# Bidirectional minGRU stack, fusion and ternary FFN on one Trainium2 core: first pair reordered, VectorE's order in the fusion slots turned round, the last projections done tile by tile

## The chip, the cores and the metric

The kernel runs on one core of a Trainium2 chip, in one launch. The metric is the device time in microseconds; below its value in repeated runs is given as a median. A separate profiled execution gave the span, the rows and the waits that are quoted. TensorE is called PE, VectorE DVE, ScalarE ACT, GpSimd POOL and SyncE SP.

## What is computed

The input x is 8 batches of 512 tokens by 512 features, float32. Each batch goes through two stacks of four minGRU layers, one reading the tokens forward and one backward. A layer computes a gate and a candidate by matrix products, and a linear scan over the tokens; from the second layer on the input is added, and each layer ends in a LayerNorm over the features:

```python
def _mingru(x, Wz, bz, Wh, bh):
    z = jax.nn.sigmoid(jnp.einsum('bsi,hi->bsh', x, Wz) + bz)
    h_tilde = jnp.tanh(jnp.einsum('bsi,hi->bsh', x, Wh) + bh)
    a = jnp.clip(1.0 - z, CLAMP_LO, CLAMP_HI)
    return _linear_scan(a, z * h_tilde)          # h[s] = a[s] * h[s-1] + z[s] * h_tilde[s]
```

The two results are put side by side, multiplied by a fusion matrix (512 by 1024), a bias is added, and the batch's own x is added to it. The input of the stacks is the LayerNorm of x over the features. The FFN behind it is

```python
    h = jnp.einsum('btd,hd->bth', layernorm_no_affine(x), absmean(W_fc))     # ternary weights
    h = layernorm(jax.nn.gelu(h, approximate=False), ln_w, ln_b)
    return x + jnp.einsum('bth,dh->btd', h, absmean(W_proj))
```

(shortened here), where `absmean` divides a matrix by its mean absolute value and rounds to -1, 0 or 1. It has 2048 hidden features, and the output is 8 by 512 by 512.

The call of the stacks passes the same matrix and bias for gate and candidate and for both directions, so a layer of a stream needs one product per 128 features.

## The kernel before, in words

**First part, the recurrence (lines 200 to 720).** The batches are worked off in four pairs (b, b+1); a pair has four streams s = (batch, direction), and each of the layers 1 to 3 is done for the four streams in turn. Features lie on the partitions, in four chunks `o` of 128. For one chunk, PE makes `u` (line 416, four float32 matmuls of 128x512, in one of four `ps_u` buffers), ACT makes a, t and z (`factors`, lines 433 to 435), DVE clamps a (439), multiplies z and t (440), scans (444) and adds the input (496). Layer 0 (`first_layer`, lines 449 to 479) is shared by the two directions: its `u` is scaled by a row of token scales (466), and DVE runs both the forward scan zf and the backward scan z.

A LayerNorm (`norm`) needs token statistics, so PE transposes a stream to tokens by features (`pt`, line 293, one of two `ps_t` buffers), DVE takes bn_stats (149) and two or three small operations (151, 155, 160), POOL takes a power (156), ACT makes `nmr` (166) and the normalised `tok` (167), which frees the `ps_t` buffer; PE then transposes back (`pf`, line 302, one of two `ps_f` buffers), and ACT applies gamma and beta (308). After layer 3 only the scale is needed, and the chain ends with the statistics (`norm_last`). `norm_x` takes the statistics of x itself.

**Who goes when.** The order of every engine is written by a small planner. `slot(work, cap)` is one time step: the PE work given to it; due "factors"; then `shares(cap)`, which takes pieces from the queue `turns` (transpose and statistics) and from the queue `backs` (transpose back), up to two of each, the second only where `cap` is 2 or it is late; then the statistics of x (`x_shares`); due "scans"; the work's own end; due "resid"; and the functions that the shares left for the end (ACT's `tok` and affine). `now` counts slots. Each engine runs what it is given in order.

**The first pair** starts with `norm_x`, the products that center the first weights (`pm`), eight slots of `first_layer` for batches 0 and 1, and two slots with `fold_sums` (`pfold`, line 611). After layer 1 of the batch 1 streams come slots of their own for `fold` (`pm`, line 627, and four DVE multiplies of the fusion weights, line 632) and `fold_bias` (`pb`, line 638).

**A fusion stage** ends each pair (`fusion`, lines 514 to 545). For each of four token tiles DVE adds the bias row to x (525), PE makes `pu` of both directions (530, eight matmuls), and DVE adds both to it, scaled by the tokens' rs (538); SP stores the row. Between the tiles stand the first layers of the next pair. A list `extra` holds pieces of the weights' quantisation, two DVE operations each (171 and 172); in the fusion stages `pieces(1 + t % 2)` works one or two off after each tile's slot. `combined` (line 597) splits the two FFN LayerNorm rows in four DVE operations, when the last pair starts.

**Second part, the FFN (from line 742).** For each batch and each of 16 hidden chunks k, `fc` makes eight matmuls (781), ACT the GELU (785), a square (787) and a scaled copy (789), and DVE two sums (796) and the rest `glo` (798); `proj` follows two chunks behind (808, eight matmuls into four `po` tiles). After the last chunk `token_stats` (819 to 831) reduces the sums to a token scale; for the last batch four `center` operations (841) and four final ones (854) on DVE end the work, and SP stores each tile.

Of the kernel before, what the change touches and what calls it, by code (L numbers as in the profile page):

```python
# [24 lines left out]
def kernel(  # L25
# [90 lines left out]
    nc.vector.memset(warm, 0.0)  # L116

# [7 lines left out]
    load_xT(1)  # L125
    for t in range(NT):
        load_x("n", 1, t)
    nc.sync.dma_start(out=gam, in_=gamma)
# [78 lines left out]
    with rec:  # L207
# [28 lines left out]
        def shares(cap):  # L236
# [3 lines left out]
            for q in (turns, backs):  # L240
                some = []
                for i in range(2):
                    if not q or not ready(q[0][0]):
                        break
                    at, piece = q[0][:2]
                    late = (at.at if isinstance(at, Tokens) else at) + piece < now[0]
                    if i >= cap and not late:
                        break
                    some.append(take(q))
                last = some + last  # L250
# [36 lines left out]
        def turned(zs, t, name, frees=0):  # L287
            def source():
                if t == NT - 1:
                    zlive[0] -= frees  # L290
                pt = ps_t.tile([P, H], F32, tag="pt", name=f"pt_{name}")
# [25 lines left out]
        def norm(s, zs, tag, pause):  # L317
# [8 lines left out]
            for t in range(NT):  # L326
                queue(turns, s, at, t, tokens(turned(zs, t, f"{tag}_{t}", NC_), toks, None, f"{tag}_{t}"))
            for c in range(NC_):
                queue(backs, s, toks, c, back(toks, dst, c, True, f"{tag}_{c}"))
# [69 lines left out]
        def slot(work=None, cap=1):  # L399
            end = work() if work is not None else None  # L400
            due("factors")
            last = shares(cap) + x_shares()
# [43 lines left out]
        def first_layer(b, lag=0):  # L446
# [4 lines left out]
            def chunk(o):  # L451
                def work():
# [11 lines left out]
                    def scaled():  # L464
# [4 lines left out]
                        def scans():  # L469
# [3 lines left out]
                            scan(z, a, z, True)  # L473
                            zf.append(f)
                            zb.append(z)
                            if o == NC_ - 1:
                                state[b, 0] = xT.pop(b)
                                norm((b, 0), zf, f"{b}0_0", 1)
                                norm((b, 1), zb, f"{b}1_0", 1)
# [5 lines left out]
        def layer(s, l):  # L485
# [5 lines left out]
            for o in range(NC_):  # L491
# [14 lines left out]
                if s[0] < 2 and (l == L - 1 or o % 2) and len(extra) > 2 * NW:  # L506
# [8 lines left out]
        def fusion(b):  # L515
            hs, rs = [], []

            def tile_of(t):
                def work():
# [5 lines left out]
                    nc.vector.tensor_tensor(row, row, fb, ALU.add)  # L525
                    pus = []
# [69 lines left out]
        def combined():  # L596
# [3 lines left out]
            for i, v in enumerate((lnw, lnb)):  # L600
                hi, lo = rows["comb"][:, :, 2 * i, :], rows["comb"][:, :, 2 * i + 1, :]
                v = v.unsqueeze(2).broadcast_to([P, NF, 32])
                nc.vector.tensor_copy(hi, v)
                nc.vector.tensor_tensor(lo, v, hi.bitcast(F32), ALU.subtract)


        def fold_sums(d):
# [7 lines left out]

            def end():
                folded[d] = tokp.tile([P, H], F32, tag="tok", name=f"fold_{d}")
                held[0] += 1
                nc.scalar.copy(folded[d], ps)
            return end  # L620

        folded = {}

        def fold(d):
# [3 lines left out]

            def end():
                for c in range(NC_):  # L630
                    w = fw[:, d * NC_ + c, :]
                    nc.vector.scalar_tensor_tensor(w, w, gam[:, c : c + 1], pm, ALU.mult, ALU.subtract)
            return end

        def fold_bias():
# [3 lines left out]

            def end():  # L640
                nc.vector.tensor_tensor(fb, pb, fb, ALU.add)
                held[0] -= 2
            return end
# [7 lines left out]
        for b in range(2):  # L651
            norm_x(b, 0)
# [10 lines left out]
        both = const.tile([P, NC_, 2, 64], F32, name="both")  # L663
        picks = []
        for i in range(2):
            s = const.tile([P, P], F32, name=f"fpick{i}")
            nc.vector.memset(s, 0.0)
            nc.vector.memset(s[64 * i : 64 * i + 1, :], 1.0 / H if i else 1.0)
            picks.append(s)
        f0, f1 = first_layer(0), first_layer(1, 2)  # L670
        for work in f0:
            slot(work, 2)
        for i, v in enumerate((bet, gam)):
            nc.vector.tensor_copy(both[:, :, i, :], v.unsqueeze(2).broadcast_to([P, NC_, 64]))
        for work in f1:
            slot(work, 2)
        for d in range(2):
            slot(lambda d=d: fold_sums(d), 2)
        for b in range(0, B, 2):
# [11 lines left out]
            for l in range(1, L):  # L691
# [5 lines left out]
                for s in ((b, 0), (b, 1), (b + 1, 0), (b + 1, 1)):  # L697
# [12 lines left out]
                    if s[0] == 1 and l == 1:  # L710
                        slot(lambda d=s[1]: fold(d))
                        if s[1] == 1:
                            slot(fold_bias)
# [5 lines left out]
            for i in range(2):  # L719
                for t, tile_ in enumerate(fusion(b + i)):  # L720
                    slot(tile_, 2)
                    pieces(1 + t % 2)
# [14 lines left out]

    gpool = ctx.enter_context(tc.tile_pool(name="g", bufs=3, reuse_waits="tile"))
    partp = ctx.enter_context(tc.tile_pool(name="parts", bufs=4, reuse_waits="tile"))
# [63 lines left out]
    def proj(b, k, *parts):  # L803
        if k == 0:
            po[b] = [ps_o.tile([P, H], F32, tag=f"po{t}", name=f"po_{b}_{t}") for t in range(NT)]
        for t in range(NT):
# [41 lines left out]
    def finish(b):  # L848

        for t in range(NT):  # L850
            rs = stat[b][0][:, t : t + 1]
            if b == B - 1:
                row = xs["y", b, t]
                nc.vector.scalar_tensor_tensor(row, po[b][t], rs, row, ALU.mult, ALU.add)
                store(b, t)
            else:
                scaled = tokp.tile([P, H], F32, tag="tok", name=f"scaled_{b}_{t}")
                nc.scalar.activation(scaled, po[b][t], AF.Copy, scale=rs)

                def rest(t=t, scaled=scaled):  # L860
                    center(b, t, scaled)
                    store(b, t)
                rests.append(rest)
# [15 lines left out]
    for j in range(B * NF + LAG):  # L879
        b, k = divmod(j, NF)  # L880
        late = []
        if b < B:
            waiting.append((b, k, *fc(b, k)))
# [16 lines left out]
        if b < B:  # L900
            at = 12 if b == 0 else 8
            if at <= k < at + NT:
                xt = xs["y", b, k - at]
                nc.vector.tensor_tensor(xt, xt, rows[1], ALU.add)
            if b + 1 < B:
                if k == 2:
                    load_y(b + 1)
                if k in (6, 7):
                    y_stats(b + 1, (2 * k - 12, 2 * k - 11))
                if k in (8, 9):  # L910
# [44 lines left out]
```

## Time and profile before

| what | value |
|---|---|
| time, median of 3 runs | 1756.46 us (1756.12 to 1757.0) |
| the profiled execution: its time | 1756.91 us |
| its span in the profile | 1754.9 us |
| PE busy | 1713.5 us (98%) |
| DVE busy | 1456.2 us (83%) |
| ACT busy | 1068.7 us (61%) |
| POOL busy | 214.7 us (12%) |
| PE waits for ACT's `tok` before `pt` | 14.4 us in 14 waits |
| PE waits for ACT's `tok` before `pf` | 4.5 us in 3 waits |

A row of the timeline gives the start, the length in us, the engine, the line, the operation, what it writes and reads, the number of records that it holds, and in brackets the engine's idle time before it with the instruction that ended it. A line of the waits gives the engine, the line that waited, what it waited for, the time in all, how often, and the longest. A busy engine is not an engine at its peak: matmuls overlap, and their pace is read from their starts.

### The profile page before, as it was taken

The page shows a single profiled execution, that of the slowest core. Times are in us where ns is not written, and L with a number is a line of the kernel's source. Part 1 is how long each engine was busy: PE and PEld are TensorE (multiplying, and loading weights), DVE is VectorE, ACT ScalarE, POOL GpSimd, SP SyncE. Part 2 cuts the span into 40 slices and gives each one's busy share as a digit, 9 for nine tenths or more (in the row PEclk, how much of TensorE's full clock was granted, in tenths as well). Part 3 has the DMA queues.
Part 4 walks back from the last instruction along what each step waited for, and adds up shares of the span by engine and source line. Part 5 has one row for each costly group of instructions (what it writes and reads, how often), then busy time and mean ns, then how long its engine had stood idle before and what let it go on. Part 6 is the DMA issues. An engine that isn't in the chain of part 4 may idle for free.

```text
span 1754.9 us, 19733 instructions
## 1 busy us (share of the span) xinstructions
PE 1713.5 (98%) x6424; PEld 1043.4 (59%) x6424; DVE 1456.2 (83%) x2865; ACT 1068.7 (61%) x1836; POOL 214.7 (12%) x334
## 2 busy tenths in 40 slices
PE   7989999999999999999999999999999999999998
PEld 3544554455555445555544455554588888888886
DVE  6988989789998988999898899997468778778876
ACT  3887884248887335888623588871256566566653
POOL 1111112111111111111111111111000000000000
PEclk9999999999999999999999999999999999999999
DMA  7002321132000024100002301101301101101100
GB/s 264 13 25 72 102 73 43 54 110 107 1 1 24 19 78 155 61 1 5 20 31 84 114 1 48 73 1 50 119 0 49 42 7 48 49 13 36 49 24 24
DMA packets 46454, 91.73 MB, mean 52 GB/s; under 512 B 5264, under 2 KB 5264, under 8 KB 45328
## 3 DMA queue, kind: packets, MB, share of 16 engines
q1 hardware_dynamic: 45488, 88.91, 15.0%
q10 hardware_dynamic: 864, 1.57, 0.3%
q8 instruction: 50, 0.82, 0.2%
q14 instruction: 52, 0.43, 0.1%
HBM read 65.30 MB, written 25.17 MB: 52 GB/s over the span
## 4 chain that ended last, share of the span: by engine, by line
PE 82%; DVE 10%; issue 4%; ACT 2%; POOL 1%; DMA 0%; DVEq 0%; POOLq 0%
PE u L416 33%; PE ph L781 12%; PE po L808 11%; PE pu L530 11%; PE pt L293 5%; PE u L459 4%; PE pf L302 4%; DVE st L149 2%; DVE z L444 2%; DVE z L440 1%; PE py L192 1%; DVE zf L444 1%; DVE mv L151 1%; ACT tok L167 1%; DVE z L496 1%
## 5 line engine op out<-in xcount | busy, mean ns | idle before, releaser
L416 PE MATMUL u<-xT,gw 128*128 128x512 f32 x768 | 348.8, 597 | 0.0
L416 PE MATMUL u<-h,gw 128*128 128x512 f32 x768 | 346.5, 594 | 0.0
L444 DVE TENSOR_TENSOR_SCAN z<-a,z 128x512 f32<-128x512 f32 x224 | 274.3, 1224 | 7.8
L785 ACT ACTIVATE g<-ph 128x512 f32<-128x512 f32 x128 | 76.4, 597 | 245.6 <-PE ph L781 245.6
L433 ACT ACTIVATE a<-u,ngb 128x512 f32<-128x512 f32 x192 | 131.7, 686 | 153.7 <-PE u L416 152.6
L149 DVE BATCH_NORM_STATS2 st<-pt 128x6 f32<-128x512 f32 x256 | 177.7, 694 | 56.1 <-PE pt L293 55.4
L416 PEld LDWEIGHTS u<-xT,gw 128*128 128x128 f32 x768 | 139.8, 192 | 139.8 <-issue 139.8
L416 PEld LDWEIGHTS u<-h,gw 128*128 128x128 f32 x768 | 139.0, 191 | 138.3 <-issue 138.3
L156 POOL TENSOR_TENSOR rs<-ve,mhalf 128x1 f32<-128x1 f32 x192 | 122.9, 640 | 724.5 <-DVE nmu L160 671.6
L808 PE MATMUL po<-pwq,ghi 128*128 128x512 f32 x512 | 203.5, 397 | 0.0
L781 PE MATMUL ph<-yhi,fcq 128*128 128x512 f32 x512 | 199.7, 390 | 0.0
L808 PE MATMUL po<-pwq,glo 128*128 128x512 f32 x512 | 199.6, 390 | 0.0
L781 PE MATMUL ph<-ylo,fcq 128*128 128x512 f32 x512 | 199.4, 389 | 0.0
L440 DVE TENSOR_TENSOR z<-z,t 128x512 f32<-128x512 f32 x224 | 153.8, 687 | 16.0 <-ACT z L435 15.7
L167 ACT ACTIVATE tok<-pt,nmr,rs 128x512 f32<-128x512 f32 x192 | 149.2, 777 | 6.4
L796 DVE TENSOR_TENSOR acc<-acc,g 128x512 f32<-128x512 f32 x112 | 77.3, 691 | 91.0 <-ACT g L785 90.1
L293 PEld LDWEIGHTS pt<-ident,z 128*128 128x128 f32 x640 | 78.2, 141 | 92.6 <-issue 43.8
L435 ACT ACTIVATE z<-u,gb 128x512 f32<-128x512 f32 x192 | 132.1, 688 | 0.0
L434 ACT ACTIVATE t<-u,gb 128x512 f32<-128x512 f32 x192 | 130.6, 680 | 0.0
L433 ACT ACTIVATE a<-z,ngb 128x512 f32<-128x512 f32 x32 | 23.1, 721 | 166.8 <-DVE z L466 166.6
L302 PE MATMUL pf<-ident,tok 128*128 128x128 f32 x768 | 115.0, 274 | 6.5 <-ACT tok L167 4.5
L459 PE MATMUL u<-xT,gw 128*128 128x512 f32 x256 | 117.3, 605 | 2.2 <-DVE xf L538 1.8
(138 smaller groups left out, 2650.0 us busy)
## 6 DMA issues: line engine op xcount, KB each, us to landing
xn<-in_x_dram SPq DMA_DIRECT2D x32, 256.0 KB, 5.5
xf<-in_x_dram SPq DMA_DIRECT2D x32, 256.0 KB, 5.8
x<-xf SPq DMA_DIRECT2D x32, 256.0 KB, 2.0
xy<-x SPq DMA_DIRECT2D x32, 256.0 KB, 3.7
out_dram<-xy SPq DMA_DIRECT2D x32, 256.0 KB, 2.0
xT<-in_xt_dram SPq DMA_DIRECT2D x7, 1024.0 KB, 7.7
fca<-in_fc_wT_dram SPq DMA_DIRECT2D x16, 256.0 KB, 3.0
pwa<-in_proj_wT_dram SPq DMA_DIRECT2D x16, 256.0 KB, 2.7
```

What stands on the lines that cost most here:

```text
L149: nc.vector.bn_stats(st, src)
L167: nc.scalar.activation(dst, src, AF.Identity, bias=nmr, scale=rs)
L293: nc.tensor.transpose(pt[:, ts(c, P)], zs[c][:, ts(t, P)], ident)
L302: nc.tensor.transpose(pf[:, ts(t, P)], toks[t][:, ts(c, P)], ident)
L416: nc.tensor.matmul(u, lhsT=gw[l][:, c, ts(o, P)], rhs=h[:, c, :], start=(c == 0), stop=(c == NC_ - 1),)
L433: nc.scalar.activation(a, u, AF.Sigmoid, bias=ngb[:, l, o : o + 1], scale=-1.0)
L440: nc.vector.tensor_tensor(z, z, t, ALU.mult)
L444: nc.vector.tensor_tensor_scan(dst[:, d], a[:, d], z[:, d], 0.0, ALU.mult, ALU.add)
L459: nc.tensor.matmul(u, lhsT=gw[0][:, c, ts(o, P)], rhs=xT[b][:, c, :], start=(c == 0), stop=(c == NC_ - 1),)
L530: nc.tensor.matmul(pu, lhsT=hs[d][:, c, ts(t, P)], rhs=fw[:, d * NC_ + c, :], start=(c == 0), stop=(c == NC_ - 1),)
L781: nc.tensor.matmul(ph, lhsT=w, rhs=ys[b][c][i], start=(c == 0 and i == 0), stop=(c == NC_ - 1 and i == 1),)
L808: nc.tensor.matmul(po[b][t], lhsT=part[:, ts(t, P)], rhs=pwq[k // NP_][:, k % NP_, :], start=(k == 0 and i == 0), stop=(k == NF - 1 and i ...
```

## The change

No arithmetic is added or removed. Five groups of edits move work:

- First pair: the memsets of `both` and `picks` come first; batch 1's x is loaded before its transposed copy; two of batch 1's statistics are taken before the first slot; both batches' first layers are one loop, with cap 4 in one slot; batch 0's backward scans run one slot later than the forward ones; the norms of these two batches are planned two pieces to a slot; two transposes use `ps_f`; and the fold's products and multiplies lose their own slots and are put beside layers 1 and 2.
- Fusion slots: the quantisation pieces stand inside the tile's work, and in `slot(..., long=True)` the due scans and the tile's own end come before the shares.
- A piece counts as late one slot sooner in `shares`, which can take more than two.
- The four operations of `combined` become pieces for the last pair's layer 3.
- The last four FFN chunks are drawn together; the token statistics of the last batch stand ahead of projection 12, and the last two projections are done token tile by token tile, each followed by its final operation and store. `parts` gets five buffers instead of four.

```diff
@@ shares
-                for i in range(2):
+                for i in range(max(2, cap)):
...
-                    late = (at.at if isinstance(at, Tokens) else at) + piece < now[0]
+                    late = (at.at if isinstance(at, Tokens) else at) + piece <= now[0]
@@ turned
-                pt = ps_t.tile([P, H], F32, tag="pt", name=f"pt_{name}")
+                spare = name.startswith("00_0") and t > 1
+                pt = (ps_f if spare else ps_t).tile([P, H], F32, tag="pf" if spare else "pt", name=f"pt_{name}")
@@ norm
-                queue(turns, s, at, t, tokens(turned(zs, t, f"{tag}_{t}", NC_), toks, None, f"{tag}_{t}"))
+                queue(turns, s, at, t // pair, tokens(turned(zs, t, f"{tag}_{t}", NC_), toks, None, f"{tag}_{t}"))
...
-                queue(backs, s, toks, c, back(toks, dst, c, True, f"{tag}_{c}"))
+                queue(backs, s, toks, c // pair, back(toks, dst, c, True, f"{tag}_{c}"))
@@ slot
-        def slot(work=None, cap=1):
+        def slot(work=None, cap=1, long=False):
             end = work() if work is not None else None
             due("factors")
+            if long:
+                due("scans")
+                end()
+                end = None
             last = shares(cap) + x_shares()
             due("scans")
@@ first_layer
                             scan(f, a, z, False)
-                            scan(z, a, z, True)
                             zf.append(f)
...
+                            def backward():
+                                scan(z, a, z, True)
+                                zb.append(z)
+                                if o == NC_ - 1:
+                                    norm((b, 1), zb, f"{b}1_0", 1, 2 if b < 2 else 1)
+                            if b == 0:
+                                stages.append((now[0] + 1, "resid", backward))
+                            else:
+                                backward()
@@ layer
-                if s[0] < 2 and (l == L - 1 or o % 2) and len(extra) > 2 * NW:
+                if s[0] < 2 and (l == L - 1 or o % 2) and len(extra) > 2 * NW or s[0] + 2 >= B and l == L - 1:
                     pieces(1)
@@ fusion
                     nc.vector.tensor_tensor(row, row, fb, ALU.add)
+                    pieces(1 + t % 2)
@@ combined
-                nc.vector.tensor_copy(hi, v)
-                nc.vector.tensor_tensor(lo, v, hi.bitcast(F32), ALU.subtract)
+                extra.append([None, lambda hi=hi, v=v: nc.vector.tensor_copy(hi, v)])
+                extra.append([None, lambda hi=hi, lo=lo, v=v: nc.vector.tensor_tensor(lo, v, hi.bitcast(F32), ALU.subtract)])
@@ fold
-            def end():
-                for c in range(NC_):
+            for c in range(NC_):
+                def chunk(c=c):
                     w = fw[:, d * NC_ + c, :]
                     nc.vector.scalar_tensor_tensor(w, w, gam[:, c : c + 1], pm, ALU.mult, ALU.subtract)
-            return end
+                stages.append((now[0] + c, "resid", chunk))
@@ first pair
-            norm_x(b, 0)
+            norm_x(b, -2)
...
-        for work in f0:
-            slot(work, 2)
+        for _ in range(2):
+            take(xturns)
+        for i, work in enumerate(f0 + f1):
+            slot(work, 4 if i == NC_ + 1 else 2)
...
-        for d in range(2):
-            slot(lambda d=d: fold_sums(d), 2)
...
-                    if s[0] == 1 and l == 1:
-                        slot(lambda d=s[1]: fold(d))
-                        if s[1] == 1:
-                            slot(fold_bias)
+                    if b == 0 and l == 1 and s[0] == 0:
+                        fold_sums(s[1])
+                    if b == 0 and l == 2:
+                        if s[0] == 0:
+                            fold(s[1])
+                        elif s[1] == 0:
+                            fold_bias()
@@ fusion stage
-                    slot(tile_, 2)
-                    pieces(1 + t % 2)
+                    slot(tile_, 2, True)
@@ end of the FFN
+    def finish_last(b, t):
+        row = xs["y", b, t]
+        nc.vector.scalar_tensor_tensor(row, po[b][t], stat[b][0][:, t : t + 1], row, ALU.mult, ALU.add)
+        store(b, t)
...
-    for j in range(B * NF + LAG):
+    for j in range(ends):
...
-        if b < B:
-            waiting.append((b, k, *fc(b, k)))
+        for _ in range(2 if ends - 4 <= j < ends - 2 else 1):
+            if todo:
+                waiting.append((*todo[0], *fc(*todo[0])))
+                todo.pop(0)
+        if j == ends - 2:
+            late.append(token_stats(b))
...
+    for t in range(NT):
+        for done in waiting:
+            proj(*done, tiles=(t,))
+        finish_last(B - 1, t)
```

## The prediction

> **What bounds the kernel now.** I read five views: the totals and the chain that ended last, the waits of TensorE (PE), a table of windows by stage, and the timelines of PE and VectorE (DVE) around each gap of PE.
>
> ```profile
> span 1754.9 us, 19733 instructions
> PE 1713.5 (98%) x6424; PEld 1043.4 (59%) x6424; DVE 1456.2 (83%) x2865; ACT 1068.7 (61%) x1836; POOL 214.7 (12%) x334
> PE 82%; DVE 10%; issue 4%; ACT 2%; POOL 1%; DMA 0%; DVEq 0%; POOLq 0%
> PE pt L293 <- ACT tok L167: 14.4, 14, 2.4
> PE pf L302 <- ACT tok L167: 4.5, 3, 2.6
> PE pt L293 <- DVE zf L444: 3.5, 1, 3.5
> PE u L459 <- DVE xf L538: 1.8, 1, 1.8
> 20.00:160.00 140.00, 125.98 (x447) 67.84 (x446) 119.28 (x246) 100.36 (x178) 20.06 (x33) 0.95 0.15 52
> 640.00:700.00 60.00, 57.16 (x189) 28.93 (x187) 50.10 (x100) 28.48 (x49) 7.86 (x12) 0.97 0.38 123
> ```
>
> PE is the bound: 1754.9 - 1713.5 = 41.4 us of idle in all. Nothing is removed from PE by this change, so it can win only from this idle time, and from the stretches at half clock that follow some of it (a group of four matmuls starts every 0.43 us per matmul, and every 0.85 at half clock). The waits say what is late: the token chain (bn_stats on DVE, pow on POOL, `nmr` and `tok` on ACT), which frees one of only two `ps_t` buffers. In the window rows the columns after the length are PE, PEld, DVE, ACT and POOL busy, then the granted clock. The first 160 us hold 19.3 us of PE idle (14.0 of it after 20), at a clock of 0.95. The three fusion stages with first layers in them (320 to 400, 640 to 700, 940 to 1020) hold 4.84, 2.84 and 5.12; the last 15 us hold 8.1; the rest 1.2.
>
> **First pair.** Three things change. (a) DVE gets the first forward scan of chunk 3 sooner: four backward scans (1.15 each from issue to issue) of batch 0 wait a slot, two statistics of batch 1 (1.02 each) go into DVE's idle time before 15.67, and the memsets go to the front. I walked DVE's row durations through the new order: zf_0_3 comes at 33.4 where it ended at 36.85, so the 3.51 us wait nearly goes. (b) Two turns and two backs per slot, and the `ps_f` spares, let PE reach its first layer-1 matmul (L416) at about 48.1 against 61.0: 12.9 earlier. Of that 6.87 (16 pfold matmuls, 0.43 each) is work only moved to later, and 0.87 other order: net 5.2. New waits of 1.7 and 1.0 for late scans are inside the 48.1. (c) DVE was nearly full here (119.3 of 140), so PE, now ahead, waits for it: by the walk 0.8, 0.9, 0.25, 3.0 (batch 1's transposes wait for its last forward scan), 0.9, 0.6 and 0.6, 7.05 in all. In the same stretch before, 0.43 and 1.96 of waits and 1.56 of half clock fall away. At the layer-1 group that started at 109.05 the gain is 5.2 - 7.05 + 3.95 = 2.1.
>
> (d) The fold slots. They give PE two or four matmuls while a whole slot's chain must be waited for, and their 2.71 us of DVE multiplies stand ahead of the next slot:
>
> ```profile
> 121.12 0.65 PE L293 MATMUL pt<-ident,z 128*128 128x128 f32 x4 [2.43 <-ACT tok L167]
> 149.92 0.47 PE L302 MATMUL pf<-ident,tok 128*128 128x128 f32 x1 [2.61 <-ACT tok L167]
> ```
>
> Counted from start to start, with the half clock after each, these two places cost 2.59 + 0.76 + 0.84 and 0.66 + 2.77 + 1.53 = 9.15. Put beside ordinary layer slots (4.3 us of PE, 4.0 to 4.3 of DVE with statistics) and with one 0.68 us multiply per slot, the fold has cover; without it I would expect one of the two back. I take all 9.15, less 0.9 for a half-clock window after the new 3.0 wait (the mean price of such a window here is (0.84 + 1.56 + 0.84 + 1.53 + 1.64) / 5 = 1.3, times 0.7): first pair -10.3, range -6 to -13.
>
> The DMA queue: SP now issues four xn of batch 1 (1 MB, 2.6 us at the 390 GB/s of this stretch) before xT of batch 1. The xn land near 12.4 to 14.1, in time for the early statistics; xT(1) lands near 17, needed at 26. Hidden. In the fusion slots the staged loads and quantised stores move ahead of the x1 stores; x1 is read a stage later, also hidden.
>
> **Fusion slots.** Here the order on DVE turns round: pieces, scans, the two adds of the fusion, and only then statistics. These rows are of the second fusion stage:
>
> ```profile
> 636.89 1.04 PE L293 MATMUL pt<-ident,zf 128*128 128x128 f32 x8
> 641.20 0.60 PE L293 MATMUL pt<-ident,zf 128*128 128x128 f32 x4
> 651.10 0.66 PE L293 MATMUL pt<-ident,z 128*128 128x128 f32 x4 [1.99 <-ACT tok L167]
> ...
> 637.53 0.70 DVE L149 BATCH_NORM_STATS2 st<-pt 128x6 f32<-128x512 f32 x1 [0.25 <-PE pt L293]
> 643.28 1.51 DVE L538 SCALAR_TENSOR_TENSOR xf<-pu,rsv,xf 128x512 f32<-128x512 f32 x2
> 644.71 0.48 DVE L171 TENSOR_SCALAR fcq<-fcb,lo_fc 128x512 f32<-128x512 f32 x1
> 647.67 0.69 DVE L149 BATCH_NORM_STATS2 st<-pt 128x6 f32<-128x512 f32 x1
> ...
> 639.76 0.78 ACT L167 ACTIVATE tok<-pt,nmr,rs 128x512 f32<-128x512 f32 x1
> ```
>
> What it takes away: the pieces no longer hold up the statistic at 647.67, so the 1.99 (2.0 to 2.2 with its row's spacing) goes; in the first fusion stage the tile of the threshold `pth` also goes through `ps_u` earlier, and the 1.84 wait of u for the adds goes. What it adds: the first statistic of the next batch's zf started 0.6 us after its transpose, at 637.53; its `tok` freed the buffer at 640.54, 3.0 us on, and PE asked for it at 641.20. After the change two pieces (2 x 1.18), a group of clamp, product and two scans (3.46) and the two adds (1.45) are ahead. Walked from 626.15: group to 631.7 - 635.16, add of fb 635.76, pieces 638.12, group 641.58, adds 643.03, then the statistic, and `tok` frees the buffer at 646.05. PE, with a wait of some 0.9 of the same kind one transpose earlier, arrives at 642.05: a new wait of 4.0. Behind pt_0_2 in PE's queue stand the next tile's eight `pu` matmuls, so nothing covers it. Once this pair of buffers is late, the following transposes arrive late too and wait no more. Per stage, without clock: first +4.0 - 2.0 - 2.2 and about -0.5 of smaller differences = -0.7; second +4.0 - 2.0 - 1.6 (the half clock at 651.6 was paid) + 1.0 = +1.4; third +4.0 + 0.9 - 2.1 - 2.2 = +0.6, the last term being combined's four DVE operations (992.98 to 995.1), which stood ahead of a statistic that PE waited 2.38 for. Sum +1.3.
>
> The clock: does a wait of 4.0 bring half clock? The row first: after 1.99 idle, PE's matmuls from 651.59 were at half speed for one window of 3.41 and lost 1.64; after 2.38 at 995.9 nothing was lost. So the trace gives half clock when enough idle falls in one window, and 4.0 is twice what sufficed. The Trainium skill, "TensorE: Matmul & The Clock Gate", section "Why this matters for your kernels", says that gaps above about 3 us, one window of idle, bring the clock back to half. Taken as one whole idle window of 3.41, a wait of 4.0 covers one only when it begins in the first 0.6 of it, about 1 time in 6: nearly nothing. By the rows it is 1.3 to 1.4 a stage, +4.2, of which about 1.0 is absorbed in waits behind. I take the row: fusion +1.3 + 3.2 = +4.5. By the page it is +1.5. Bounds: -7 (no new wait, all old ones gone) to +9.
>
> **Combined pieces** add 1.1 us at most to four DVE slots of the last pair (about 4.6 against PE's 4.3); covered by slack before and after, 0 to +0.5. I take 0.
>
> **End.**
>
> ```profile
> 1746.45 2.74 DVE L841 SCALAR_TENSOR_TENSOR xy<-row,nmrg,xy 128x512 f32<-128x512 f32 x4
> 1746.49 0.39 PE L808 MATMUL po<-pwq,glo 128*128 128x512 f32 x1
> 1749.11 2.72 DVE L854 SCALAR_TENSOR_TENSOR xy<-po,rsg,xy 128x512 f32<-128x512 f32 x4
> ```
>
> Four centers and four finals are in series on DVE after the pow, and the last PE matmul is already done at 1746.9. After the change fc 12 to 15 are drawn together and the statistics stand ahead of projections 12 to 15. The last sums then come two projections (2 x 8 x 0.228 = 3.65) earlier on PE, less about 0.4 for ACT's five operations of two chunks; the reduction starts near 1739.8 instead of 1743.04, and `nmr` is out 3.4 later as before, at 1743.2; centers end at 1746.1, the finals, tile by tile behind PE, at 1748.8 instead of 1751.83: -3.0 (range -2.5 to -3.3); the last store still takes its 2 us.
>
> **Sum.** -10.3 + 4.5 + 0 - 3.0 = -8.8 on the profiled span of 1754.9: 1746.1. The profiled execution took 1756.91, so 2.0 lie around the span, and it was 0.45 above the median of 1756.46. 1746.1 + 2.0 - 0.5 = 1747.6; I say 1747.5.
>
> **Rivals.** A change within 0.2%, 3.5 us, can hardly be told from none, so faster is under 1752.95 and slower above 1760.
>
> A, no new wait in the fusion stages: the statistic's delay is met by PE coming later too, or DVE is ahead of my walk. For it: DVE idles 55.4 us over the kernel waiting for `pt`. Against it: it did not idle in the 15 us before 637. Fusion -6 instead of +4.5: 1737.
>
> B, the change of the first pair does not do what it says: DVE, with 119.3 of 140 us busy and the same work, sets the end of that stage, and PE's waits only move. For it: the walk already turns 12.9 into 2.1 at 109. Against it: the fold's 9.15 lie in slots where PE had nothing else. First pair -3: 1755.
>
> C, slower: the late statistics in the fusion stages carry on from tile to tile, since two buffers serve all turns. One wait is 4.0; if each of the other three tiles of a batch brought 2 more, a stage would cost 6 more, and three stages 18: 1765. It decides from where the fusion stages lose over 16.8 in all (13.3 gained elsewhere, and 3.5), 5.6 each. Against it: behind the first wait PE is late and DVE idle again.
>
> **From this the numbers.** Likeliest case 0.52, its own range 1743 to 1752; A 0.26; B 0.15; C 0.07. Range for 8 in 10: 1736.5 to 1755.5, from A's fastest to B. Faster: 0.51 of the likeliest, all of A and a quarter of B, 0.81; same 0.12; slower 0.07.
>
> **What would show it.** First L416 matmul near 48; no gap of PE over 1 us between 110 and 150; in each of three fusion stages one gap of about 4 us before the third transpose of zf, and the clock at half behind it; the gaps at 649 and 996 gone; the four finals of the end starting near 1746 minus what is gained ahead of it, directly behind the centers, and the span ending about 6 us behind their start. Wrong if the fusion gaps are absent (then A), or repeated (C), or if gaps before 110 sum to much more than 12.

## The result

The changed kernel takes 1748.76 us (median of 6 runs, 1747.81 to 1748.87) against 1756.29 (median of 6) before: a ratio of 0.9957 with a 95% interval of 0.9944 to 0.9969, so 7.5 us or 0.43% faster. The forecast was 1747.5, in a range of 1736.5 to 1755.5. The profiled execution took 1748.87, with a span of 1746.9: 8.0 less than the 1754.9 of before, where the sum of the steps said 8.8.

First the totals and two stretches of the changed kernel, from its page and its table of windows (length; PE, PEld, DVE, ACT and POOL busy; granted clock; DMA share; GB/s):

```profile
span 1746.9 us, 19727 instructions
PE 1713.6 (98%) x6424; PEld 1043.8 (60%) x6424; DVE 1453.2 (83%) x2865; ACT 1067.8 (61%) x1836; POOL 217.1 (12%) x334
20.00:160.00 140.00, 133.54 (x482) 71.66 (x481) 122.94 (x254) 110.29 (x199) 21.43 (x33) 0.98 0.21 72
600.00:700.00 100.00, 95.40 (x305) 48.28 (x304) 82.59 (x164) 41.77 (x70) 11.95 (x19) 0.97 0.39 126
```

PE does the same 1713.6 us of work. Between 20 and 160 its idle time fell from 14.0 to 6.5, and the clock there rose from 0.95 to 0.98. Around the second fusion stage idle time grew: 4.6 us of these 100, where before 2.84 lay between 640 and 700 and none in the 40 us ahead.

The waits of PE in the changed kernel (engine, line, what it waited for; us in all, times, longest):

```profile
PE pt L301 <- ACT tok L174: 12.9, 8, 3.9
PE pt L301 <- DVE zf L457: 3.9, 1, 3.9
PE pf L310 <- ACT tok L174: 2.3, 4, 1.4
PE pt L301 <- DVE z L457: 1.2, 1, 1.2
```

The wait for `tok` at the transposes made 14.4 us in 14 pieces before; now it makes 12.9 in 8, so there are fewer and longer ones. Three of them are the new ones of the fusion stages, 3 x 3.87 = 11.6 of the 12.9.

Where the time went is best read as a lead: the start of a given matmul in the profile of before, less its start in the profile of a later kernel. A stage that keeps the lead runs as fast as before. One execution each; two of them can differ by 1 to 2.5 us in the first pair alone, in part through the clock (the spare-buffer run has no half clock there and leads by 13.4 at the first `pu`; the changed kernel has 6.83 us of it and leads by 10.9).

| kernel | first L416 | first `pu` | layer 2 of pair 2 | of pair 3 | of pair 4 | first FFN matmul | span |
|---|---|---|---|---|---|---|---|
| before, start at | 61.00 | 284.96 | 454.13 | 756.90 | 1060.43 | 1255.88 | 1754.9 |
| changed | 13.0 | 10.9 | 10.6 | 7.1 | 5.9 | 4.5 | 8.0 |
| old slot order | 13.4 | 11.5 | 10.9 | 11.0 | 11.1 | 9.7 | 13.3 |
| statistics before scans | 13.0 | 11.1 | 16.1 | 20.1 | 25.1 | 23.7 | 27.3 |
| spare buffer | 13.7 | 13.4 | 14.1 | 12.9 | 12.8 | 11.4 | 14.9 |
| filler, 6.86 us | 13.1 | 12.1 | 10.4 | 6.5 | 3.7 | 2.3 | 5.9 |
| filler, 3.44 us | 13.8 | 12.0 | 13.0 | 12.0 | 12.0 | 10.6 | 14.2 |
| combined in last fusion | 13.4 | 11.5 | 11.3 | 8.0 | 6.7 | 6.8 | 10.4 |
| end alone | -0.2 | -1.3 | -1.2 | -1.2 | -1.2 | -1.3 | 2.3 |
| first pair alone | 12.4 | 11.6 | 9.7 | 8.4 | 6.5 | 6.6 | 6.6 |
| slot order alone | 0.4 | 0.8 | -0.8 | -3.2 | -5.7 | -5.5 | -5.5 |
| fold in own slots | 13.9 | 7.5 | 5.8 | 2.1 | 0.6 | -0.8 | 2.8 |
| combination | 4.0 | 6.3 | 11.4 | 15.4 | 20.4 | 20.6 | 24.1 |
| combination 2 | 13.4 | 12.3 | 17.4 | 21.3 | 26.3 | 26.5 | 30.0 |

The changed kernel's row tells the whole: the first pair wins 10.9, the three fusion stages give back 0.3, 3.1 and 1.3 (and 0.3 between the stages), the last pair 1.4, and the end wins 3.5.

### The profile page after: what moved, and what is told of

Same layout as the page of the kernel before. It is cut to its first block, busy times and chain, and to the rows that moved or that the text cites. A ratio compares the mean times of both kernels' runs of the same rounds, so it can differ in the third digit from the quotient of the medians.

```text
span 1746.9 us, 19727 instructions
## 1 busy us (share of the span) xinstructions
PE 1713.6 (98%) x6424; PEld 1043.8 (60%) x6424; DVE 1453.2 (83%) x2865; ACT 1067.8 (61%) x1836; POOL 217.1 (12%) x334
## 4 chain that ended last, share of the span: by engine, by line
PE 72%; DVE 21%; issue 4%; ACT 2%; POOL 0%; DMA 0%; DVEq 0%; POOLq 0%; ACTq 0%
PE u L429 27%; PE ph L790 12%; PE po L817 11%; PE pu L551 9%; DVE z L457 5%; PE pt L301 4%; PE pf L310 4%; DVE st L156 3%; DVE z L453 2%; PE u L472 2%; DVE zf L457 1%; DVE a L452 1%; DVE xf L559 1%; DVE mv L158 1%; PE py L199 1%
## 5 line engine op out<-in xcount | busy, mean ns | idle before, releaser
L429 PE MATMUL u<-xT,gw 128*128 128x512 f32 x768 | 345.4, 593 | 0.0
L173 ACT ACTIVATE nmr<-nmu,rs 128x1 f32<-128x1 f32 x192 | 56.7, 295 | 103.7 <-POOL rs L163 101.2
L551 PE MATMUL pu<-fw,xT 128*128 128x512 f32 x256 | 119.6, 611 | 0.0
```

The lines of the kernel that those rows point to most:

```text
L429: nc.tensor.matmul(u, lhsT=gw[l][:, c, ts(o, P)], rhs=h[:, c, :], start=(c == 0), stop=(c == NC_ - 1),)
L551: nc.tensor.matmul(pu, lhsT=hs[d][:, c, ts(t, P)], rhs=fw[:, d * NC_ + c, :], start=(c == 0), stop=(c == NC_ - 1),)
```

## The experiments

All kernels compute the whole output. The times are medians of repeated runs, the ratios those to the kernel before on the same chip.

**The old order in the fusion slots.** The changed kernel with only this undone:

```diff
-                    slot(tile_, 2, True)
+                    slot(tile_, 2)
+                    pieces(1 + t % 2)
```

(and the call of `pieces` inside the tile's work taken out).

> The changed kernel with the fusion slots as they were before (statistics, then scans, adds, and the pieces behind the slot); all other parts of the change stay. Theory (late statistics hold two ps_t buffers): the three new waits of 3.9 and the half clock behind them go, and the old waits of about 2 each come back. From the start of the first fusion stage to the first group behind the third the change lost 10.87 - 5.86 = 5.0, in spite of about 2.2 won by moving combined; without the new order about 5 + 2 is won back: 1742, between 1740 and 1744. Rival (the order of VectorE in these slots is about neutral, the waits only change places): 1748 to 1749.

Measured: 1743.64 us, ratio 0.992 (0.9907 to 0.9932). The theory's number. The waits of 3.9 are gone and the old ones of about 2 (2.15 from start to start) are back, so this part of the change costs 5 to 6 us where it stands (the lead at the FFN is 9.7 against 4.5).

**Only the statistics moved ahead.**

```diff
-                    slot(tile_, 2, True)
+                    slot(tile_, 2)
```

(the pieces stay inside the tile's work, so DVE does pieces, statistics, scans, adds).

> The changed kernel with VectorE's order in a fusion slot: pieces, statistics, scans, adds. Only the statistics move, 3.46 + 1.45 = 4.9 earlier than in the changed kernel. Theory: the first tok frees its ps_t buffer near 1 us ahead of PE, all three waits of 3.9 go, and with them the half clock (1.1, 2.1 and 1.1 us): 16 us, so about 1732.5, between 1730 and 1737. Rival (VectorE has no room in these slots, so what is moved ahead makes the scans late and PE waits for those instead): 1744 to 1749.

Measured: 1729.42 us, ratio 0.9836 (0.9822 to 0.9849), 27.8 us less than before on its chip. That is a little under the theory's range: 19 us won against the changed kernel, where 16 were forecast. The three waits (4.0 each from start to start) and the half clock behind them (5.0 by the filler run below) make 17; the other 2 stay open. Here are the timeline rows that decide it (start, length, engine, line, operation), first of the changed kernel:

```profile
322.46 1.04 PE L301 MATMUL pt<-ident,zf 128*128 128x128 f32 x8
323.33 3.60 PE L472 MATMUL u<-xT,gw 128*128 128x512 f32 x8
330.80 1.11 PE L301 MATMUL pt<-ident,zf 128*128 128x128 f32 x4 [3.87 <-ACT tok L174]
331.71 4.73 PE L551 MATMUL pu<-fw,xT 128*128 128x512 f32 x8
...
326.26 1.58 DVE L559 SCALAR_TENSOR_TENSOR xf<-pu,rsv,xf 128x512 f32<-128x512 f32 x2
327.75 0.69 DVE L156 BATCH_NORM_STATS2 st<-pt 128x6 f32<-128x512 f32 x1
...
329.97 0.78 ACT L174 ACTIVATE tok<-pt,nmr,rs 128x512 f32<-128x512 f32 x1
```

and the same place with the statistics ahead:

```profile
322.25 1.04 PE L301 MATMUL pt<-ident,zf 128*128 128x128 f32 x8
323.13 3.60 PE L472 MATMUL u<-xT,gw 128*128 128x512 f32 x8
326.80 0.66 PE L301 MATMUL pt<-ident,zf 128*128 128x128 f32 x4
...
323.75 0.69 DVE L156 BATCH_NORM_STATS2 st<-pt 128x6 f32<-128x512 f32 x1
...
329.48 1.51 DVE L559 SCALAR_TENSOR_TENSOR xf<-pu,rsv,xf 128x512 f32<-128x512 f32 x2
```

In the changed kernel the transpose is ready at 323.5, its statistic starts at 327.75 behind the adds, and PE stands from 326.9 to 330.8. In the other the statistic starts at 323.75, and PE goes on at 326.80. The scans and adds, now 3 us later, are waited for by nobody. Both the new wait and the old one of 2 behind the pieces are gone, and that in all three stages: the lead grows by 5.0, 4.3 and 5.0 in them.

**A spare buffer for the third transpose.**

```diff
-                spare = name.startswith("00_0") and t > 1
+                spare = name.startswith("00_0") and t > 1 or name[1:4] == "0_0" and name[0] in "246" and t == 2
```

> The changed kernel with its order on VectorE, but the third transpose of zf of batches 2, 4 and 6 takes a ps_f buffer, so that it need not wait for the first tok. Theory (the buffer is what PE waits for, not the statistic itself): the three waits of 3.9 and their half clock go without any move on VectorE, 12 + 4.3: about 1732.5, and no less than 10 us won. Rival (the late statistic is waited for anyway, one transpose later or at the transposes back): 1744 to 1749.

Measured: 1745.94 us (1741.98 to 1747.32), ratio 0.9931 (0.9917 to 0.9944). The theory wanted 10 us or more; the time is the rival's, and the timeline shows its mechanism:

```profile
324.29 0.60 PE L301 MATMUL pt<-ident,zf 128*128 128x128 f32 x4
331.59 0.60 PE L301 MATMUL pt<-ident,zf 128*128 128x128 f32 x4
339.08 2.18 PE L301 MATMUL pt<-ident,z 128*128 128x128 f32 x8 [3.02 <-ACT tok L174]
...
336.07 0.69 DVE L156 BATCH_NORM_STATS2 st<-pt 128x6 f32<-128x512 f32 x1
```

The third transpose (324.29) no longer waits, but the statistic of the fourth (336.07) stands behind the scans and adds of the next tile in turn, and PE waits 3.0 one tile further on. So what was recorded as "the buffer is what PE waits for" is too simple: here the buffer moved the wait, and the earlier statistic removed it.

**A filler in the wait, to ask the clock.** Eight matmuls ahead of the waiting transpose, into a `ps_f` tile that nobody reads:

```diff
+                if name[1:] == "0_0_2" and name[0] in "246":
+                    fill = ps_f.tile([P, S], F32, tag="pf", name=f"fill_{name}")
+                    for c in range(8):
+                        nc.tensor.matmul(fill, lhsT=ident, rhs=zs[c % NC_], start=(c == 0), stop=(c == 7))
```

> The changed kernel with eight more matmuls of 128x512 (8 x 0.43 = 3.4 us, into a ps_f buffer that nobody reads) ahead of the third transpose of zf of batches 2, 4 and 6, where PE waits 3.9 us. Theory (the half clock behind these waits comes from PE's idle time): PE is idle for only 0.5 there, the half clock at these three places goes, 1.1 + 2.1 + 1.1: about 1744.5, with a granted clock of 1.00 there. Rival (the half clock comes with the place, the kind of work or the time, not with idle): 1748.5 to 1749.

Measured: 1751.1 us, ratio 0.9963 (0.995 to 0.9975). A float32 matmul of the source is two records, so the filler took 6.86 us, not 3.4, and its time says nothing against the theory; the granted clock was 1.00 in all three places. Four matmuls instead of eight:

> The changed kernel with the filler ahead of the third transpose of zf of batches 2, 4 and 6, now of half the length: it turned out that each matmul of the source is two records, so the first filler took 6.86 us where PE waits 3.87, and cost 3.0 a stage; here it takes 3.44. Theory (the half clock comes from the idle time): PE idles 0.5 there, granted clock 1.00 in the three stages, and 1.1 + 2.1 + 1.1 less than the changed kernel, less what a later wait of some 0.6 takes back: 1745 to 1746.5. Rival (the half clock is there with or without idle time; or it is absorbed in full by waits behind it): 1748 to 1749.

Measured: 1742.76 us, ratio 0.992 (0.9906 to 0.9933), on the theory's side and below its range; the rival falls. From the windows around the second stage, of the changed kernel:

```profile
630.00:650.00 20.00, 16.13 (x41) 7.57 (x41) 15.12 (x34) 6.45 (x12) 3.15 (x5) 0.83 0.24 75
```

and with the filler of 3.44:

```profile
630.00:650.00 20.00, 19.16 (x63) 9.44 (x62) 17.06 (x43) 10.99 (x20) 4.64 (x7) 1.00 0.18 66
```

The filler does no useful work and delays nothing, since PE still waits 0.6 behind it (from start to start), but the clock stays at 1.00 instead of 0.83. From the first `pu` of pair 1 to the first FFN matmul the lead falls by 1.4 instead of 6.4: the half clock behind the three waits is worth 5.0 us of the changed kernel's time.

**Combined elsewhere.**

```diff
-                if s[0] < 2 and (l == L - 1 or o % 2) and len(extra) > 2 * NW or s[0] + 2 >= B and l == L - 1:
+                if s[0] < 2 and (l == L - 1 or o % 2) and len(extra) > 2 * NW:
```

> The changed kernel, but the four operations of combined are worked off in the last pair's fusion slots instead of its layer 3. Theory (in layer 3 they stand in four slots that also carry the statistics of y, so VectorE needs about 5.0 a slot against PE's 4.3, and PE waits 1.4 and 0.4 at 1152): both waits go, 1.4 to 1.8 us less than the changed kernel: 1747.2. Rival (these waits come from the statistics of y and not from combined): no change, 1748.8.

Measured: 1746.48 us, ratio 0.9939 (0.9927 to 0.9952). The lead no longer falls in the last pair (6.7 and 6.8), so the rival falls. What stood there in the changed kernel, from its timeline:

```profile
1146.16 0.68 DVE L625 TENSOR_TENSOR comb<-lnb,comb 128x512 fp32r<-128x512 f32 x1
1146.76 0.69 DVE L156 BATCH_NORM_STATS2 st_y<-xy 128x6 f32<-128x512 f32 x1
1150.68 0.69 DVE L156 BATCH_NORM_STATS2 st<-pt 128x6 f32<-128x512 f32 x1
...
1153.84 0.33 PE L310 MATMUL pf<-ident,tok 128*128 128x128 f32 x1 [1.41 <-ACT tok L174]
```

Each of the four slots carries a statistic of a stream (1.15), one of y (1.15), the scan group (2.2) and a piece (0.3 to 0.6): 4.8 to 5.05 us from one stream statistic to the next on DVE in the first three, against 4.3 of PE, and after the fourth the statistic at 1150.68, which the last transpose back needs, is late.

**The end alone**, on the kernel before (its second part taken whole from the changed one):

```diff
+        if j == ends - 2:
+            late.append(token_stats(b))
...
+    for t in range(NT):
+        for done in waiting:
+            proj(*done, tiles=(t,))
+        finish_last(B - 1, t)
```

> The kernel before with the changed end alone. Theory: the gain of the changed kernel's last 50 us, 8.0 of the span less 4.45 at its first FFN matmul, is that part's own: 3.5 us less than before, 1752.8, with PE's first FFN matmul where it was. Rival (part of it comes with the state in which the FFN starts): 1 to 2 us less.

Measured: 1753.37 us, ratio 0.9982 (0.9975 to 0.9989). In its profile PE is 1.3 behind at the FFN and the span 2.3 ahead, so the end itself wins 3.5, as in the changed kernel. The lines of the end of the changed kernel that answer to those shown of before:

```profile
1735.01 1.28 DVE L829 TENSOR_REDUCE su<-pst 128x4 f32<-128x512 f32 x2
1738.41 2.74 DVE L850 SCALAR_TENSOR_TENSOR xy<-row,nmrg,xy 128x512 f32<-128x512 f32 x4
1742.09 0.39 PE L817 MATMUL po<-pwq,glo 128*128 128x512 f32 x1
1741.07 2.72 DVE L871 SCALAR_TENSOR_TENSOR xy<-po,rsg,xy 128x512 f32<-128x512 f32 x4
```

Centers and finals are still 5.4 us in series on DVE, and the last matmul now falls among the finals, at 1742.09, instead of 2.6 us ahead of them.

**The first pair alone**: the changed kernel with the fusion slots, combined and the end as before.

```diff
-                    pieces(1 + t % 2)
...
-                    slot(tile_, 2, True)
+                    slot(tile_, 2)
+                    pieces(1 + t % 2)
```

(shortened: combined and the whole second part are put back in the same way).

> The kernel before with the changed first pair alone (fusion slots, combined and end as before). Theory: the first fusion matmul comes 10.9 us earlier, and nothing of it is lost later, since the stages behind have their own waits: 1745.5. Rival (a lead is given back where the later stages wait on transfers or on VectorE): 1749 to 1754.

Measured: 1748.61 us, ratio 0.9953 (0.9939 to 0.9966), between the theory and the rival. The lead of 11.6 at the first fusion is there, but only 6.6 of it reach the FFN: the theory's "nothing is lost later" does not hold. The old waits in the fusion stages are as long as before (2.15 from start to start), but behind all three of them PE now runs four or five matmuls at half clock, where the profile of before has this behind one; and the wait at the third stage's end, behind combined, is 2.8 instead of 2.4. The run with the old slot order in the changed kernel has the half clock behind one of three again. So the same wait costs 2.2 or, with the half clock (5.3 us for eight matmuls that take 3.6), about 3.8; which it is depends on where it falls, as the last section shows. In the lead the difference is smaller: 2.0 are lost in the first and the third stage, 1.0 in the second, where before has the half clock too, and what makes up these 1.0 was not taken apart.

**The slot order alone**, on the kernel before:

```diff
+            if long:
+                due("scans")
+                end()
+                end = None
...
-                    slot(tile_, 2)
-                    pieces(1 + t % 2)
+                    slot(tile_, 2, True)
```

> The kernel before with the new order in the fusion slots alone. Theory: the three waits of 3.9 come with their half clock, the old waits of about 2 go; in the changed kernel this and the moved combined (2.2 won) made 5.0 of loss, so alone about 7 us more than before: 1763, between 1760 and 1765. Rival (the loss in the changed kernel came only from the lead of PE over VectorE that the first pair gives): 1755 to 1757.

Measured: 1762.07 us, ratio 1.003 (1.0019 to 1.0041): 5.5 slower and within the theory's range. The three waits of 3.9 each are there without any lead of PE, so the rival falls. One of them:

```profile
647.36 1.12 PE L293 MATMUL pt<-ident,zf 128*128 128x128 f32 x4 [3.87 <-ACT tok L167]
```

**The fold in slots of its own again**, in the changed kernel:

```diff
+                    if s[0] == 1 and l == 1:
+                        slot(lambda d=s[1]: fold(d))
+                        if s[1] == 1:
+                            slot(fold_bias)
```

(and their calls beside layer 2 taken out; the four multiplies stand together in the slot again).

> The changed kernel with the fold and the fold bias in slots of their own again, after layer 1 of batch 1's streams (the pfold products stay where the change put them). Theory (the waits in these slots are worth 9.15, and come back with them): the lead over the kernel before at the first fusion matmul falls from 10.9 to about 1.7, so 1757 to 1758; with half of the waits covered by the two-a-slot plan, 1753. Rival (the first pair's gain comes from the earlier scans and the layout of the norms, and the fold is covered anyway): 1748.8 to 1750.

Measured: 1752.39 us, ratio 0.9977 (0.9967 to 0.9987), the case "half of the waits covered". Against the run with the short filler, which has the same first 100 us (leads of 13.9 and 13.8), the lead at the first fusion matmul is 7.5 instead of 12.0: the fold's own slots are worth 4.5 in the new plan, with waits of 0.96 and 2.40 from start to start and a stretch of half clock behind the second, some 1.7 us:

```profile
140.21 0.33 PE L310 MATMUL pf<-ident,tok 128*128 128x128 f32 x1 [2.23 <-ACT tok L174]
140.38 2.56 PE L656 MATMUL pb<-fold,fpick 128*128 128x512 f32 x4
```

(Four such matmuls take 1.88 at full clock.)

**Two combinations.** The first takes the statistics ahead of the scans, combined in the last fusion, and the first `pfold` ahead of layer 1 of the first stream:

```diff
+                    if b == 0 and l == 1 and s == (0, 0):
+                        fold_sums(0)
                     layer(s, l)
-                    if b == 0 and l == 1 and s[0] == 0:
-                        fold_sums(s[1])
+                    if b == 0 and l == 1 and s == (0, 1):
+                        fold_sums(1)
```

> The changed kernel with three edits: statistics between pieces and scans in the fusion slots (run e2_stats_before_scans), combined in the last fusion (run e5_combined_in_last_fusion), and the first pfold product ahead of layer 1 of the first stream, where it stands before the wait of 3.9 at 64.5 instead of behind it. Theory: 19.3 + 1.7 of the first two, and 3.4 of the wait with about 1 to 2 of half clock from the third: 1724 to 1725, with no wait of PE over 1.6 us. Rival for the third edit (VectorE sets the end of that stretch, and the wait only moves): 1727.

Measured: 1735.13 us, ratio 0.9876 (0.9861 to 0.9891), 8 us or more above both the theory and the rival. The third edit is a loss of about 5 us (the lead at the first fusion matmul is 6.3, against 11.1 with the statistics ahead alone), which the timeline explains:

```profile
51.40 0.29 DVE L683 COPY both<-gam 128x256 f32<-128x256 f32 x1
...
51.74 5.40 PE L634 MATMUL pfold<-fw,both 128*128 128x512 f32 x8 [4.44 <-DVE both L683]
```

The product reads two small copies that DVE makes behind its backlog of scans, so PE stands 4.4 us and then runs at half clock. The second combination puts the product before the last chunk of that layer, behind those copies:

```diff
+                if s == (0, 0) and l == 1 and o == NC_ - 1:
+                    fold_sums(0)
                 slot(gates(h, l, o, f"{s[0]}{s[1]}_{l}_{o}", scans))
```

> The changed kernel with the same first two edits as e11_combination (statistics between pieces and scans; combined in the last fusion), but the first pfold product ahead of the last chunk of layer 1 of the first stream, near 61, where the copies that it reads have been done for 9 us (they ended near 51.6 in e11_combination, and the product waited 4.4 for them). Theory: the wait of 3.9 at 64.5 shrinks to about 1 and the half clock behind it goes, 4 us, on top of 19.3 + 1.6: 1723.5 to 1725. Rival (VectorE sets the end of this stretch, so the wait comes later): 1727 to 1728.

Measured: 1726.51 us, ratio 0.9822 (0.9809 to 0.9835), the fastest of all, 30.8 us under the kernel before on its chip. The time lies between the theory's range and the rival's. On the third edit the rival has the mechanism: the wait of 3.9 is gone, but the next transposes wait 2.9, as DVE sets the pace of this stretch:

```profile
68.34 0.77 PE L301 MATMUL pt<-ident,zf 128*128 128x128 f32 x5 [0.44 <-DVE zf L457]
75.42 0.66 PE L301 MATMUL pt<-ident,zf 128*128 128x128 f32 x4 [2.88 <-ACT tok L174]
```

At the first fusion matmul the lead is 12.3, against 10.9 to 13.4 in kernels without this edit, so it is worth little.

## Why the prediction was right, and where it was not

**First pair.** The sum said -10.3, and the lead at the first fusion matmul is 10.9. Place by place: the first L416 matmul was put at 48.1 and came at 47.98; the waits ahead of it, put at 1.7 and 1.0, measured 1.25 and 0.34, with one of 0.39 between them; the wait for batch 1's last forward scan, put at 3.0, measured 3.88:

```profile
47.98 3.60 PE L429 MATMUL u<-xT,gw 128*128 128x512 f32 x8
68.70 1.33 PE L301 MATMUL pt<-ident,zf 128*128 128x128 f32 x5 [3.88 <-DVE zf L457]
69.82 5.96 PE L634 MATMUL pfold<-fw,both 128*128 128x512 f32 x8
```

Behind it the clock was at half: `pfold` took 5.96 for what takes 3.6, 2.4 us more, and the transposes ahead of it 0.6 more, where 0.9 was set down for all. Two terms were off and cancelled: the lead at the group of 109.05 was put at 2.1 and is -0.1, and the 9.15 of the fold slots became 11.0 from there to the first fusion. Only 4.5 of this is due to the fold having no slots of its own (shown by putting them back); the rest goes with the other changes of the plan there, the planner's earlier "late" among them, which were not told apart.

**Fusion slots.** This step was right in its mechanism, place and size. Forecast was one new wait of 4.0 at the third transpose of zf in each of three stages; measured 3.87 each. Forecast for the stages with the clock was +4.5; the lead falls by 0.3, 3.1 and 1.3, 4.7 in all. Taking the row and not a whole idle window for the clock was the better choice. The Trainium skill ("TensorE: Matmul & The Clock Gate", section "Why this matters for your kernels") counts one window of idle. Four profiles have these waits: the changed kernel, combined in the last fusion, the slot order alone, and the fold in own slots. Of their twelve waits only four (two of them in the changed kernel) hold a whole clock step of 3.41 without work of PE, yet all twelve are followed by half clock, over two to six matmuls. Read simply as a gap above about 3 us, the page fits these waits too, but not the half clock behind waits of 2.0 (last section). The filler gives the price: 5.0 us for three, where 4.2 were set down and 1.0 of it taken off as absorbed.

Rival A (no new wait) falls with the profile, and rival B (the first pair gives little) with the lead of 10.9 at the first fusion. Rival C (the late statistics carry on from tile to tile) does not occur in the changed kernel, but the spare-buffer run shows that it lies close: let PE past the first wait, and the next tile's statistic is late in its turn.

**Combined.** This is the step that failed: "covered by slack before and after, 0 to +0.5". It cost 1.4 us of lead, outside the bound. The slot of 4.6 us of DVE left out that the statistics of y stand in the same slots; with them it is about 5. The moved statistic of the next pair, which no longer waits behind combined, is in the third fusion stage's sum.

**End.** Forecast -3.0 (2.5 to 3.3), measured -3.5 in the changed kernel and alone. The mechanism held; the reduction started 0.3 and `nmr` came 0.4 earlier, against the lead, than was walked.

**The sum.** In the lead the parts are -10.9 for the first pair, +4.7 for the three fusion stages, +0.3 between them, +1.4 for the last pair and -3.5 for the end, -8.0 in all against -8.8. That the total came so near is in part luck: the first pair and the end won 1.1 more than was set down, and combined and the rest lost 1.9 more. The first pair's number is lucky too, since eight profiles with the same first pair lead by 10.9 to 13.4 at the first fusion.

## What to carry to other kernels

On an engine that serves a chain with two buffers, put the operation that starts the chain's longest way round (statistic, pow, normalise, buffer free) ahead of the long operations that nobody waits for; the same instructions in another order moved this kernel by 19 us. When a piece of work is put into a gap, count everything that already stands in those slots, and look up what its operands wait for. When PE must wait, price the half clock behind the wait with it.

## What the runs showed that was not expected

The clock's price is a matter of where a wait falls. Waits of 2.15 us from start to start in the fusion stages were followed by half clock in one stage of three (before, the end alone, and the old slot order) and in three of three (the first pair alone), about 1.7 us each; waits of 4.0 always were. The traces show what decides it. In every profile that has several, the stretches of half clock, leaving out the one at the end, begin whole multiples of 3.41 us apart and last 3.41 or 6.83, so the clock changes in steps of 3.41. Here are pairs of such steps (length; PE, PEld, DVE, ACT and POOL busy; granted clock; DMA share; GB/s): two waits of before, one of the first pair alone, and one wait of 3.87 of the changed kernel.

```profile
347.84:351.26 3.42, 1.61 (x7) 1.07 (x8) 2.10 (x7) 2.74 (x5) 1.17 (x2) 1.00 0.31 115
351.26:354.67 3.41, 3.41 (x16) 1.99 (x15) 3.23 (x6) 1.07 (x2) 0.66 (x1) 1.00 0.00 0
...
648.22:651.63 3.41, 1.42 (x11) 0.89 (x10) 2.15 (x9) 3.00 (x6) 1.47 (x2) 1.00 0.65 211
651.63:655.04 3.41, 3.41 (x7) 1.32 (x6) 3.07 (x7) 1.85 (x3) 0.66 (x1) 0.50 0.00 1
...
335.22:338.63 3.41, 1.43 (x10) 0.98 (x9) 2.06 (x9) 2.99 (x7) 1.47 (x2) 1.00 0.75 261
338.63:342.04 3.41, 3.41 (x6) 1.35 (x5) 3.16 (x7) 1.77 (x3) 0.65 (x1) 0.50 0.01 2
...
630.94:634.35 3.41, 1.19 (x3) 0.19 (x1) 3.17 (x8) 0.00 (x0) 0.09 (x1) 1.00 0.14 52
634.35:637.76 3.41, 1.76 (x5) 1.25 (x6) 2.03 (x6) 2.81 (x6) 1.01 (x2) 0.50 0.37 108
```

The first wait of 2.0 lies across the border of two steps, with 1.8 us of PE's idle time in the step shown, and the next step stays at full clock. The second and the third lie whole in one step (3.41 - 1.42 = 1.99), and the next step is at half. Laid over all fourteen profiles (without the first 12 and the last 15 us), each of the 36 steps at full clock with 2.0 us or more of idle PE was followed by half clock, none with less than 1.88, and 9 of the 16 in between. This is read from the traces; no run shifted a wait against the steps on purpose. It says why the same wait of 2.0 costs more in one profile than in another, and why one of 3.87, most of which falls into one step or is split in halves of nearly 2, was punished twelve times of twelve.

Idle filled with matmuls whose result nobody reads kept the clock at 1.00 and made the kernel 6 us faster (1742.76 against 1748.76, on different chips; 1.1 of it is a better first pair in that profile), though the waiting transposes came no earlier for it.
